# First attention of a two-layer kernel: quadrant matmuls in two pairs per segment, elu made up to a segment ahead

## The chip, the cores and the metric

The kernel runs on one core of a Trainium2 chip. The metric is the device time of one execution in microseconds (us). Timed runs of the kernel before gave 761.18, 761.67 and 762.66 us; the median is 761.67. The engines are called PE (TensorE, matmuls; PEld is its weight load), DVE (VectorE), ACT (ScalarE), POOL (GpSimd) and SP (SyncE, which issues DMAs).

## What is computed

Two layers on x of shape 4 x 512 x 128. Each is `x = x + attention(layernorm(x)) * silu(experts(layernorm(x)))`. The change concerns the attention of the first layer alone: 16 heads of 64, sequences cut into segments of 64 positions, with a memory M, Z carried from segment to segment:

```
scores = where(mask, -inf, q @ k^T / 8);   att_dot = softmax(scores) @ v
sq = elu(q) + 1;   att_mem = sq @ M / (sq @ Z^T)
sk = elu(k) + 1;   M += sk^T @ v;   Z += sum(sk)
out = (gate * att_mem + (1 - gate) * att_dot) @ Wo
```

q, k and v are projections of the normed x. There are 4 batches of 8 segments, so 32 segments, all 16 heads of a segment at once.

## The kernel before

A first stage norms x and runs the first layer's experts (to about 78 us). Then comes the first attention, `attn0`, until about 339 us, into which the beginning of the second layer's experts is woven (the `between` table: sums, norms, transposes `lnt`, hidden layer `pgr` and router logits `lp` after segments 18 to 23, and the first expert's `ph` in segment 31). The second layer's experts and its attention follow to the end.

**Order.** Matmuls, activations and DVE operations are pinned: each of these engines runs them in the order in which the program emits them. POOL operations and DMAs are not pinned; a scheduler places those. So the loop at the end of `attn0` is the order of PE, ACT and DVE, written by hand.

**Segment n.** The steps, each with its PSUM tile's name, which is also its name in the profile:

- `scores(n)`: 16 quadrant products (64 x 64) into `sc`; DVE takes the minimum with the causal cap into E (L656); `scores_exp` is the exponential on ACT.
- `elu_exp(n, w)`: ACT makes exp and relu of q (w = 0) or k (w = 1), 128 x 512 each (`elu`, `up`); `elu(n, w)`: DVE joins the two (L679).
- `memory(n)`: sq times memory, quadrants, into `mm`; DVE divides (L711, L712), POOL multiplies by the gate (L731).
- `update(n)`: sk times v, quadrants, into `mu`; DVE adds to the memory `mz` (L746). The last segment of a batch has none.
- `attend(n)`: E times v, quadrants, into `dot`; DVE divides and keeps the extremes of the sums (L765, L712, L768); POOL multiplies by the gate and adds the memory's part (L769, L770).
- `keys(n)`: four 128 x 128 transposes of elu(k) into `pk` (L686); ACT copies them to `sk`.
- `attended(n)`: four transposes of the result into `pa` (L780); ACT copies them in four parts to `attT`.
- `output(h)`, once in four segments: 32 products with Wo into `po`; DVE multiplies by the expert branch (`sg`, L802), POOL adds to x (L803).
- `values(n)`: two gathers from DRAM bring v into one of four buffers `vone`.

**Projections.** `project(h)` makes q, k and v of four segments in 12 chunks: four of v (`pv`, two products 128 x 512; ACT evicts to `vt`, of two buffers, DVE in the first two projections; SP stores `vt` to DRAM), then four of k and four of q (`pp`, 128 rows by 64 columns, eight products; ACT evicts to `pj`). The loop deals them out, three per segment (four in segments 0 to 2). A profile counts twice as many PE instructions as products, since these are in f32.

**PSUM.** `wide` tiles (two banks, three buffers) hold sc, mm, mu, dot and po; `narrow` tiles (one bank, two buffers) hold pp, pv, pk, pa and, from the woven-in work, lnt, pgr and lp. A matmul group that reuses a buffer waits for its eviction.

**Array shapes.** sc, mm, mu and dot use a 64 x 64 quarter of the array; pk, pa, pv and lnt the whole of it; pp 128 rows by 64 columns; po 64 rows by 128 columns.

The loop before, per segment: PE runs sc of the next segment, the output if it is due, a chunk, mm, a chunk, mu, a chunk, pk of the next segment, dot, pa of the segment before.

Of the kernel before, what the change touches and what calls it, by code (L numbers as in the profile page):

```python
# [101 lines left out]
def bc(ap, axis, n):  # L102

    shape = list(ap.shape)
    return ap.unsqueeze(axis).to_broadcast(shape[:axis] + [n] + shape[axis:])


class Kernel:
# [454 lines left out]
    def attn0(self, xnT, g0, stack, psum, between):  # L563
# [25 lines left out]
        def wide(name):  # L589

            return psum.tile([P, 2, S], F32, name=name, tag="w", bufs=3)
# [47 lines left out]
        def blocks(n, w):  # L639
            s = n % 4  # L640
            return qkv[n // 4][w][:, s * 8 : s * 8 + 8, :]

        def scores(n):

            q, k = blocks(n, 0), blocks(n, 1)
            ps = wide(f"sc{n}")
            for hp in range(4):
                for p in range(2):
                    for a in range(2):
                        self.mm1(  # L650
                            ps[halves[a], p, hp * 64 : hp * 64 + 64],
                            lhsT=k[halves[p], 2 * hp + a, :], rhs=q[halves[p], 2 * hp + a, :],
                            start=True, stop=True,
                        )
            e = pool.tile([P, 2, 4, LSEG], F32, name=f"E{n}", tag="E")
            self.vec1(nc.vector.tensor_tensor(  # L656
                e, ps[:, :, 0:256].rearrange("p x (hp c) -> p x hp c", hp=4),
                bc(bc(self.cap, 1, 4), 1, 2), ALU.min,
            ))
            seg[n]["e"] = e  # L660

        def scores_exp(n):
            e = seg[n]["e"]
            self.act1(e, e, AF.Exp, scale=1.0 / math.sqrt(DK))

        def last(n):
            return n % 8 == 7

        def elu_exp(n, w):
            t = pool.tile([P, 8, 64], F32, name=f"elu{w}{n}", tag=f"elu{w}")  # L670
            up = pool.tile([P, 8, 64], F32, name=f"up{w}{n}", tag="up")
            self.act1(t, blocks(n, w), AF.Exp)
            self.act1(up, blocks(n, w), AF.Relu)
            seg[n][w] = t, up

        def elu(n, w):

            t, up = seg[n][w]
            self.vec1(nc.vector.scalar_tensor_tensor(t, t, 1.0, up, ALU.min, ALU.add))  # L679
            seg[n][w] = t  # L680

        def turn(n, src, name):

            ps = narrow(f"{name}{n}").rearrange("p (hp c) -> p hp c", hp=4)
            for hp in range(4):
                self.pin(nc.tensor.transpose(  # L686
                    ps[:, hp], src[:, 2 * hp : 2 * hp + 2, :].rearrange("d a j -> d (a j)"),
                    self.ident,
                ))
            return ps.rearrange("p hp (x d) -> p hp x d", x=2)  # L690

        def keys(n):
            t = pool.tile([P, 4, 2, DK], F32, name=f"sk{n}", tag="sk")
            self.act1(t, turn(n, seg[n][1], "pk"), AF.Copy)
            seg[n]["sk"] = t

        def values(n):

            for p in range(2):
                src = vd[n // 4][p].rearrange("(s hp r) d -> s r hp d", s=4, hp=4)  # L700
                nc.sync.dma_start(out=vone[n % 4][:, :, p, 0:DK], in_=src[n % 4])

        def heads(ps):

            return ps[:, :, 0 : 4 * (DK + 1)].rearrange("p x (y v) -> p x y v", v=DK + 1)
# [4 lines left out]
        def divided(ps, t, r, sums):  # L710
            self.vec1(nc.vector.reciprocal(r, sums))  # L711
            self.vec1(nc.vector.tensor_tensor(t, heads(ps)[:, :, :, 0:DK], bc(r, 3, DK), ALU.mult))  # L712

        def memory(n):


            mz, sq = self.mz[(n % 8 + 1) % 2 + 1 if n % 8 else 0], seg[n][0]
            ps = wide(f"mm{n}")
            for hp in range(4):
                for p in range(2):  # L720
                    for a in range(2):
                        at = (2 * a + hp // 2) * (DK + 1)
                        self.mm1(
                            ps[halves[(a + hp) % 2], p, at : at + DK + 1],
                            lhsT=sq[halves[p], 2 * hp + a, :], rhs=mz[halves[p], hp, a, :],
                            start=True, stop=True,
                        )
            t = seg[n]["t1"] = pool.tile([P, 4, 2, DK], F32, name=f"t1{n}", tag="t1")
            r = pool.tile([P, 2, 4], F32, name=f"rm{n}", tag="rm")
            divided(ps, t.rearrange("p hp y d -> p y hp d"), r, heads(ps)[:, :, :, DK])  # L730
            nc.gpsimd.tensor_mul(t, t, self.gate)  # L731
# [16 lines left out]
        def attend(n):  # L748


            e, v = seg[n]["e"], vone[n % 4]
            ps = wide(f"dot{n}")
            for u in range(2):
                for p in range(2):
                    for hp in (2 * u, 2 * u + 1):
                        for a in range(2):
                            at = (2 * u + p) * (DK + 1)
                            self.mm1(
                                ps[halves[(a + hp) % 2], a, at : at + DK + 1],
                                lhsT=e[halves[a], p, hp, :], rhs=v[halves[a], hp, p, :],  # L760
                                start=True, stop=True,
                            )
            both = pool.tile([P, 2, 2, 4], F32, name=f"rd{n}", tag="rd")
            sums = both[:, 0]
            self.vec1(nc.vector.tensor_scalar_max(sums, heads(ps)[:, :, :, DK], SUM_MIN / 2))  # L765
            t = pool.tile([P, 4, 2, DK], F32, name=f"t2{n}", tag="t2")
            divided(ps, over(t), both[:, 1], sums)
            self.vec1(nc.vector.tensor_tensor(self.sums0, both, self.sums0, ALU.max))  # L768
            nc.gpsimd.tensor_mul(t, t, gate2)  # L769
            nc.gpsimd.tensor_add(t, t, seg[n]["t1"])  # L770
            seg[n]["att"] = t

        def attended(n):

            if n % 4 == 0:

                attT[n // 4] = pool.tile([P, 16, 4, 32], F32, name=f"attT{n}", tag="attT")
            ps = narrow(f"pa{n}").rearrange("p (hp c) -> p hp c", hp=4)
            for hp in range(4):
                self.pin(nc.tensor.transpose(  # L780
                    ps[:, hp, :], seg[n]["att"][:, hp].rearrange("i p v -> i (p v)"),
                    self.ident,
                ))
            src = ps.rearrange("p (a u) (h t c) -> p c a u h t", a=2, h=2, c=16)
            dst = attT[n // 4][:, :, n % 4].rearrange("p c (u y t) -> p c u y t", u=2, y=4)
            for h in range(2):
                for a in range(2):
                    self.act1(dst[:, :, :, (a + h) % 2 * 2 + a], src[:, :, a, :, h], AF.Copy)
# [16 lines left out]
        nseg = 8 * B  # L805
        for n in range(nseg):
            seg[n] = {}
        todo = project(0)
# [11 lines left out]
        scores(0)  # L820
        scores_exp(0)
        elu(0, 0)
        for n in range(nseg):
            if n == 0 or n % 4 == 3:
                todo = project((n + 1) // 4 + 1)
                each = 3 if n else 4
            nxt = n + 1 < nseg
            more = nxt and not last(n + 1)
            if n + 2 < nseg:
                values(n + 2)  # L830
            if more:
                elu_exp(n + 1, 1)
            if nxt:
                scores(n + 1)
            if n % 4 == 1 and n > 4:
                output(n // 4 - 1)
            for chunk in todo[:1]:
                chunk()
            if more:
                elu(n + 1, 1)  # L840
            if nxt:
                scores_exp(n + 1)
            memory(n)
            for chunk in todo[1:2]:
                chunk()
            if nxt:
                elu_exp(n + 1, 0)
            if not last(n):
                update(n)
            if nxt:  # L850
                elu(n + 1, 0)
            for chunk in todo[2:each]:
                chunk()
            todo = todo[each:]
            if more:
                keys(n + 1)
            for f, *args in between.get(n - 0.5, []):
                f(*args)
            attend(n)
            if n:  # L860
                attended(n - 1)
            for f, *args in between.get(n, []):
                f(*args)
        return [lambda: attended(nseg - 1), lambda: output(2 * B - 1)]
# [1411 lines left out]
```

## Time and profile before

| | |
|---|---|
| median of three runs | 761.67 us |
| profiled execution | 761.59 us, its span on the core 759.8 us |
| PE busy | 723.9 us (95%) |
| DVE, ACT, POOL busy | 515.0, 494.5, 294.7 us |
| stage of segments 3 to 18 (115.76 to 238.06 us) | PE 120.63, DVE 74.39, ACT 86.90, POOL 68.85 us busy of 122.30 |
| segments 27 to 30 (310.90 to 334.73 us) | PE 18.22, DVE 20.37, ACT 14.51, POOL 16.64 us busy of 23.83 |
| mean granted PE clock | 0.992 |

A profile line of a group gives start, duration, engine, line, operation, output and inputs, the array rows and columns or the tile's shape, how many instructions, and in brackets how long the engine had stood idle and what ended that. L331 and L334 are helpers through which all matmuls and activations go, so groups are told by their tiles. PE ends are modelled and matmuls overlap: the distance between starts of successive groups is the time that a group takes on PE. In a table of stretches the columns are the stretch, its length, busy time (and count) of PE, PEld, DVE, ACT and POOL, then the granted clock, the DMA share and GB/s.

### The profile page before, as it was taken

How to read it: one execution, taken by the hardware profiler on the slowest of the kernel's cores; microseconds unless marked ns; L12 is line 12 of the kernel's file. 1: busy time of each engine (PE TensorE's matmuls, PEld its weight loads, DVE VectorE, ACT ScalarE, POOL GpSimd, SP SyncE). 2: the span in 40 equal slices, each digit the busy share in tenths (PEclk: the TensorE clock that was granted, in tenths of full speed). 3: DMA queues.
4: the chain of work that ended last, by engine and by line, in shares of the span. 5: the costliest groups of instructions: out<-in, count | busy, mean ns of one | idle time of the engine just before them, and what ended most of it. 6: DMA issues, size and time to landing. Idle time of an engine off the chain costs nothing.

```text
span 759.8 us, 23585 instructions
## 1 busy us (share of the span) xinstructions
PE 723.9 (95%) x10044; PEld 436.8 (57%) x10044; DVE 515.0 (68%) x1126; ACT 494.5 (65%) x800; POOL 294.7 (39%) x340
## 2 busy tenths in 40 slices
PE   8999899999999989889999999999999999999995
PEld 4666677787876857667576777433234424432244
DVE  7766375556557755874365643688888998777874
ACT  4432567668567775742433222998999799989860
POOL 7660055546555543673007004331152344140160
PEclk9999999999999998999999999999999999999999
DMA  7830423223132221100002550667684776759200
GB/s 192 149 89 0 112 87 100 58 62 97 42 89 73 57 72 31 45 3 1 1 1 71 180 127 1 138 198 185 129 233 153 167 167 199 190 123 222 56 16 17
DMA packets 77743, 74.71 MB, mean 98 GB/s; under 512 B 41936, under 2 KB 66800, under 8 KB 74560
## 3 DMA queue, kind: packets, MB, share of 16 engines
q1 hardware_dynamic: 75568, 71.98, 36.5%
q0 software_dynamic: 1488, 0.90, 0.9%
q8 instruction: 81, 1.33, 0.8%
q10 hardware_dynamic: 576, 0.26, 0.1%
q14 instruction: 30, 0.25, 0.1%
HBM read 50.04 MB, written 23.07 MB: 96 GB/s over the span
## 4 chain that ended last, share of the span: by engine, by line
PE 75%; ACT 11%; DVE 9%; DMA 2%; issue 1%; POOL 0%; SPq 0%; DVEq 0%; ACTq 0%
PE eo L331 10%; PE acc L331 9%; PE pp L331 8%; ACT e L334 7%; PE ph L331 7%; PE po L331 6%; PE s L331 3%; PE b L331 3%; PE pl L331 3%; PE pv L331 2%; PE pa L780 2%; PE mm L331 2%; PE dot L331 2%; PE mu L331 2%; PE den L331 2%; PE pg L331 2%
## 5 line engine op out<-in xcount | busy, mean ns | idle before, releaser
L334 ACT ACTIVATE e<-s 128x1024 f32<-128x1024 f32 x126 | 124.3, 1062 | 12.7 <-PE s L331 12.1
L331 PE MATMUL acc<-e,strip 128*32 128x512 f32 x1008 | 124.6, 598 | 0.3 <-DVE e L1710 0.3
L334 ACT ACTIVATE e<-e 128x1024 f32<-128x1024 f32 x106 | 109.7, 1099 | 0.0
L334 ACT ACTIVATE h<-ph 128x1024 f32<-128x1024 f32 x32 | 32.7, 1023 | 85.5 <-PE ph L331 85.5
L769 POOL TENSOR_TENSOR t<-t,gate 128x512 f32<-128x512 f32 x32 | 40.8, 1274 | 75.0 <-DVE sums L768 67.5
L331 PEld LDWEIGHTS acc<-e,strip 128*32 128x32 f32 x1008 | 28.5, 109 | 69.9 <-issue 59.2
L331 PEld LDWEIGHTS eo<-w_out,h 128*128 128x128 f32 x512 | 60.7, 192 | 12.5 <-issue 9.7
L334 ACT ACTIVATE pj<-pp 128x512 f32<-128x512 f32 x64 | 38.3, 598 | 41.2 <-PE pp L331 40.9
L331 PE MATMUL eo<-w_out,h 128*128 128x128 f32 x512 | 63.4, 277 | 1.6 <-DVE g L966 1.3
L679 DVE SCALAR_TENSOR_TENSOR elu<-elu,up 128x512 f32<-128x512 f32 x60 | 48.2, 804 | 20.4 <-ACT up L334 20.3
L331 PE MATMUL ph<-xnT,w_in 128*128 128x512 f32 x128 | 61.2, 600 | 0.0
L966 DVE SCALAR_TENSOR_TENSOR g<-eo,gw,g 128x128 f32<-128x128 f32 x112 | 31.5, 343 | 40.0 <-PE eo L331 40.0
L731 POOL TENSOR_TENSOR t<-t,gate 128x512 f32<-128x512 f32 x32 | 41.4, 1294 | 40.6 <-DVE t L712 40.5
L770 POOL TENSOR_TENSOR t<-t,t 128x512 f32<-128x512 f32 x32 | 46.1, 1441 | 2.5
L331 PE MATMUL s<-q,k 64*128 64x512 bf16 x256 | 40.8, 382 | 4.5 <-ACT e L334 2.9
L331 PEld LDWEIGHTS <-k 64*128 64x128 bf16 x256 | 8.8, 94 | 61.0 <-issue 59.1
L1550 POOL TENSOR_TENSOR pr<-pr,pr 128x512 f32<-128x512 f32 x14 | 22.6, 1636 | 41.8 <-DVE pr L1545 41.8
L334 ACT ACTIVATE elu<-pj 128x512 f32<-128x512 f32 x60 | 38.0, 633 | 0.1
L334 ACT ACTIVATE up<-pj 128x512 f32<-128x512 f32 x60 | 37.8, 631 | 0.0
L334 ACT ACTIVATE attT<-pa 128x128 f32<-128x128 f32 x128 | 25.1, 284 | 17.6 <-PE pa L780 17.6
L331 PE MATMUL pv<-l0Wv,xnT 128*128 128x512 f32 x64 | 35.6, 652 | 0.8 <-ACT vt L334 0.7
L331 PE MATMUL pp<-xnT,l0Wk 128*64 128x128 f32 x512 | 35.1, 283 | 0.7 <-ACT g L334 0.7
(290 smaller groups left out, 1520.7 us busy)
## 6 DMA issues: line engine op xcount, KB each, us to landing
vd<-vt SPq DMA_DIRECT2D x32, 256.0 KB
vone<-vd SPq DMA_DIRECT2D x64, 128.0 KB
first<-qe SPq DMA_DIRECT2D x8, 1024.0 KB
second<-qf SPq DMA_DIRECT2D x16, 512.0 KB
third<-qf SPq DMA_DIRECT2D x32, 256.0 KB
qf<-qT SPq DMA_DIRECT2D x64, 64.0 KB
k<-kd SPq DMA_DIRECT2D x16, 256.0 KB
q<-qd SPq DMA_DIRECT2D x16, 256.0 KB
```

The source lines that it names most:

```text
L331: return self.pin(self.nc.tensor.matmul(*args, **kw))
L334: return self.pin(self.nc.scalar.activation(*args, **kw))
L679: self.vec1(nc.vector.scalar_tensor_tensor(t, t, 1.0, up, ALU.min, ALU.add))
L731: nc.gpsimd.tensor_mul(t, t, self.gate)
L769: nc.gpsimd.tensor_mul(t, t, gate2)
L770: nc.gpsimd.tensor_add(t, t, seg[n]["t1"])
L780: self.pin(nc.tensor.transpose(ps[:, hp, :], seg[n]["att"][:, hp].rearrange("i p v -> i (p v)"), self.ident,))
L966: self.vec1(v.scalar_tensor_tensor(acc[b][:, k, :], eo[:, k, :], w, acc[b][:, k, :], ALU.mult, ALU.add))
L1550: self.nc.gpsimd.tensor_add(self.prod1[b, m], self.prod1[b, m], t)
```

## The change

Only the preamble and the loop of `attn0` change; no operation is added or dropped.

- mm of a segment follows sc of the next one at once, and dot follows mu at once: two pairs of quadrant groups.
- The two groups of transposes (pk, pa) come next, and the projection chunks beyond the first come last. The first chunk stays between mm and mu.
- The output moves behind that first chunk.
- Chunks per segment become 4, 4, 3, 1 (for n mod 4 = 3, 0, 1, 2) instead of 3 each.
- The exponential and relu of k are issued at the end of the segment two before, those of q at the start of the segment before; DVE's elu of k comes between E and the division of mm, elu of q right behind that division, ahead of the update's addition.

```diff
         elu(0, 0)
+        elu_exp(1, 1)
         for n in range(nseg):
             if n == 0 or n % 4 == 3:
                 todo = project((n + 1) // 4 + 1)
-                each = 3 if n else 4
+            each = 4 if n < 3 else (4, 3, 1, 4)[n % 4]
...
-            if more:
-                elu_exp(n + 1, 1)
             if nxt:
+                elu_exp(n + 1, 0)
                 scores(n + 1)
-            if n % 4 == 1 and n > 4:
-                output(n // 4 - 1)
-            for chunk in todo[:1]:
-                chunk()
             if more:
                 elu(n + 1, 1)
+            memory(n)
+            for chunk in todo[:1]:
+                chunk()
             if nxt:
                 scores_exp(n + 1)
-            memory(n)
-            for chunk in todo[1:2]:
-                chunk()
+            if n % 4 == 1 and n > 4:
+                output(n // 4 - 1)
             if nxt:
-                elu_exp(n + 1, 0)
+                elu(n + 1, 0)
             if not last(n):
                 update(n)
-            if nxt:
-                elu(n + 1, 0)
-            for chunk in todo[2:each]:
-                chunk()
-            todo = todo[each:]
-            if more:
-                keys(n + 1)
             for f, *args in between.get(n - 0.5, []):
                 f(*args)
             attend(n)
+            if more:
+                keys(n + 1)
             if n:
                 attended(n - 1)
+            for chunk in todo[1:each]:
+                chunk()
+            todo = todo[each:]
+            if n + 2 < nseg and not last(n + 2):
+                elu_exp(n + 2, 1)
             for f, *args in between.get(n, []):
                 f(*args)
```

More of the change, by code (lines that the diff above doesn't have):

```diff
@@ L830, in attn0 @@
                 values(n + 2)
+            if nxt:
+                elu_exp(n + 1, 0)
+                scores(n + 1)
             if more:
-                elu_exp(n + 1, 1)
+                elu(n + 1, 1)
+            memory(n)
+            for chunk in todo[:1]:
+                chunk()
             if nxt:
-                scores(n + 1)
+                scores_exp(n + 1)
             if n % 4 == 1 and n > 4:
                 output(n // 4 - 1)
-            for chunk in todo[:1]:
-                chunk()
-            if more:
-                elu(n + 1, 1)
             if nxt:
-                scores_exp(n + 1)
-            memory(n)
-            for chunk in todo[1:2]:
-                chunk()
-            if nxt:
-                elu_exp(n + 1, 0)
+                elu(n + 1, 0)
             if not last(n):
                 update(n)
-            if nxt:
-                elu(n + 1, 0)
-            for chunk in todo[2:each]:
-                chunk()
-            todo = todo[each:]
-            if more:
-                keys(n + 1)
             for f, *args in between.get(n - 0.5, []):
```

## The prediction

> **What bounds the kernel now.** The page first: where the time goes and whether the clock is whole.
>
> ```profile
> PE 723.9 (95%) x10044; PEld 436.8 (57%) x10044; DVE 515.0 (68%) x1126; ACT 494.5 (65%) x800; POOL 294.7 (39%) x340
> PEclk9999999999999998999999999999999999999999
> PE 75%; ACT 11%; DVE 9%; DMA 2%; issue 1%; POOL 0%; SPq 0%; DVEq 0%; ACTq 0%
> ```
>
> TensorE (PE) is busy nearly all the time and carries the chain. The first attention runs from about 92 to 339 us. Next, its timeline on PE: what counts is the distance from one group's start to the next one's, since matmuls overlap.
>
> ```profile
> 219.25 0.70 PE L331 MATMUL dot<-vone,E 64*64 64x65 f32 x32
> 219.88 0.66 PE L780 MATMUL pa<-ident,t 128*128 128x128 f32 x4
> 220.47 0.69 PE L331 MATMUL sc<-pj,pj 64*64 64x64 f32 x32
> 221.41 3.84 PE L331 MATMUL po<-l0wo,attT 64*128 64x128 f32 x64 [0.25 <-ACT attT L334]
> 225.18 1.09 PE L331 MATMUL pp<-xnT,l0Wk 128*64 128x128 f32 x16
> 226.21 0.70 PE L331 MATMUL mm<-mz,elu 64*64 64x65 f32 x32
> 226.83 1.09 PE L331 MATMUL pp<-xnT,l0Wk 128*64 128x128 f32 x16
> 227.86 0.70 PE L331 MATMUL mu<-vone,sk 64*64 64x65 f32 x32
> ...
> 262.83 0.66 PE L780 MATMUL pa<-ident,t 128*128 128x128 f32 x4
> 263.33 0.60 PE L900 MATMUL lnt<-ident,xn 128*128 128x128 f32 x4
> ...
> 310.90 0.69 PE L331 MATMUL sc<-pj,pj 64*64 64x64 f32 x32
> 311.41 0.65 PE L331 MATMUL mm<-mz,elu 64*64 64x65 f32 x32
> 311.88 0.69 PE L331 MATMUL mu<-vone,sk 64*64 64x65 f32 x32
> ```
>
> PE has next to no gaps here, so its own order is the bound. A quadrant group (64*64) takes 0.63 when another array shape follows (mm 226.21 to 226.83), but 0.51 and 0.47 when a quadrant group follows (310.90, 311.41, 311.88). Transposes: 0.59 before a quadrant group, 0.50 before another transpose (262.83 to 263.33). Elsewhere in this timeline pp takes 1.02 before another shape and 0.92 before pp; pv 1.06 and 0.96. A change of shape costs **0.09 to 0.14 us**. Third, the clock, where PE is thin, because it is cut to half after such stretches (282.9 to 289.7 and 334.1 to 337.5):
>
> ```profile
> 279.50:282.90 3.40, 2.25 (x32) 1.91 (x25) 2.38 (x7) 2.10 (x7) 1.65 (x2) 1.00 0.65 198
> 317.05:320.46 3.41, 1.89 (x76) 1.47 (x69) 3.31 (x7) 2.18 (x5) 2.73 (x2) 1.00 0.06 13
> 330.70:334.10 3.40, 1.55 (x77) 1.30 (x68) 3.07 (x7) 1.67 (x3) 2.84 (x3) 1.00 0.00 0
> ```
>
> The second number is PE's busy time: 1.55 of 3.40 brought the half clock, 1.89 did not; 2.25 did, much of it in router matmuls of 32 rows by 8 columns. Last, the releases on ACT and DVE:
>
> ```profile
> 244.49 0.60 ACT L334 ACTIVATE vt<-pv 128x512 f32<-128x512 f32 x1 [1.30 <-DMA vd<-vt]
> ```
> ```profile
> 320.90 1.49 DVE L679 SCALAR_TENSOR_TENSOR elu<-elu,up 128x512 f32<-128x512 f32 x1
> ```
>
> The evictions of v have two buffers and can wait for their store; an elu on DVE takes 1.49 instead of 0.69 when POOL multiplies at the same time.
>
> **What the Trainium skill says.** "TensorEngine Tiling (Array Packing)", Tiling Modes: changing the tiling mode, not just the tile, drains TensorE. The trace agrees, at 0.09 to 0.14. "DMA: Bandwidth & Descriptors", Anatomy of one DMA: about 2.0 us fixed per transfer, plus the bytes (there for transfers issued by GpSimd). Here the 24 stores of v from ACT (256 KB each, issued by SP) had their last packet 1.65 to 3.65 after issue, mean 2.15. "GPSIMD Engine Reference", Key points: GpSimd shares its SBUF interfaces with VectorE and contends with DVE instructions of two SBUF inputs. That is the elu at 1.36 to 1.50, while E, t and mz, which read PSUM, stay at 0.69.
>
> **The change part by part.** Call the segments of one projection S3, S0, S1, S2 (n mod 4 = 3, 0, 1, 2). Per segment, in order, with | for a change of shape: before, S0 is sc|v|mm|k|mu|k|pk|dot|pa|; after, sc mm|k|mu dot|pk pa|k k k|. Over the four segments 36 changes become 19, at about 0.1 each.
>
> *The pairs and runs alone.* With the distances above, S3 is sc 0.515, mm 0.626, v 1.056, mu 0.487, dot 0.626, pk 0.495, pa 0.495, v 0.962 twice, v 1.056 = 7.28 (6.79 where the memory's last segment has no update). S0 with pp is 7.23; S1 with the output matmuls (3.772) and two trailing chunks 10.08; S2, one chunk, 4.36 (3.87 where no keys follow). S3 and S2 occur in both forms in eight segments: 7.28 + 6.79 + 2x7.23 + 2x10.08 + 4.36 + 3.87 = 56.9. Before, eight segments take 61.15 (sc at 115.76, 176.91 and 238.06). So −4.2, in which the 0.32 that po waits for attT is gone too: mm and a chunk stand before it now.
>
> *What gives it back.* (1) pk, pa and the first trailing chunk share two PSUM buffers ("t"), so that chunk needs pk's buffer. sk starts 0.693 after pk and takes 0.597, so the chunk starts 1.35 after pk, not 0.99 (v) or 1.08 (pp): +0.36 and +0.27. Before, dot and others lay between. In eight segments 2x0.36 + 4x0.27 = 1.8. (2) S2 is so short that att(n−1), which takes POOL 1.28 + 1.3 to 1.6 after t2 on DVE, comes 0.5 to 1 late for pa of S3, and elu on DVE meets these POOL operations; walking the queues, S3 becomes 7.90 and 7.48: +0.6 over (1). (3) The last three v now come at 0.96, so the fourth eviction waits for the second one's store: vt2 starts 1.81 before the next sc, ends 0.6 later, +2.15 makes 0.95 after sc, against 0.11 without a wait. Behind it on ACT stand elu_exp of k (2 operations), of q (2), the chunk's pj, E and sk, issued 0.52 apart (elu_exp) or 0.50: sk starts at 0.95 + 0.5 + 4x0.52 + 2x0.5 = 4.55 and is done at 5.15, so the trailing chunks of S0 start at 5.2, and S0 takes 8.07 instead of 7.50: +0.57, twice. (4) The rest stays covered. One segment's operations need 4.6 on DVE (five at 0.62, the small ones 0.24, 0.20, 0.24, 0.17 and a wait) and on ACT 3.7 plus 0.5 per chunk, below PE's 7 except in S2. elu of k, now ahead of the division of mm, waits for ACT until 1.8 after sc, and pk needs it at 3.28; were it later than that, PE would wait as long. The output's sg on DVE now holds up elu of q, mz and the sums of dot until po ends (6.05 after sc); they end at 8.7, before the next sc at 10.35; its POOL addition finds POOL idle. So nothing for these.
>
> Together 56.9 + 1.8 + 0.6 + 1.1 = **60.4 against 61.15**. In n = 3 to 18 that is twice 0.7: **−1.4**.
>
> *n = 19 to 26 (72.84 us before).* At n = 22 two chunks and their changes leave, but xnT waits behind the elu_exp placed ahead of it: 9.22 becomes 7.3. At n = 23 three v now run before the router matmuls, which wait for v's buffers: 10.8 becomes 11.0. The rest as above: 7.9 + 8.07 + 10.9 + 7.3 + 11.0 + 8.07 + 10.35 + 4.36 = 67.95; the half clock cost 2.7 here (sc 1.06, pv 2.0, mm 1.08, pp 1.84 instead of 0.63, 1.06, 0.63, 1.02) and, the router matmuls being as thin as before, I leave it: 70.65, **−2.2**.
>
> *n = 27 to 30 (310.90 to 334.73, no chunks).* DVE bounds it: 5.93 per segment without a gap, two elu at 1.36 and 1.49. The pairs give nothing here. But elu of q now follows t1 at once and starts before POOL takes up that t1, so it runs first: about 0.8 instead of 1.49. 5.2 for a segment; walked through 4.97, 5.2, 7.6 (output), 4.1 = 21.9: **−2.0**. PE is then busy above half of the last window before 334, as in the one at 317, so I take the second half-clock spell as gone: **−1.7** (pa, mm and ph lost that).
>
> *n = 0 to 2.* mm(0) no longer has a v chunk ahead of it while elu of q is made (1.0 idle), and DVE, which evicts these v, is late: +0.8; then −0.2 for two segments: **+0.6**. SP's stores and gathers of v keep their number; a gather ahead of a store of v1 would delay it by up to 1 us, which the third v's slack covers. The elu_exp(1,1) ahead of the loop is the same two operations, made while ACT would wait for the next scores: nothing, or 1.0 if they delayed elu of q.
>
> Sum: −1.4 − 2.2 − 2.0 − 1.7 + 0.6 = −6.7, from the profiled 761.59 (span 759.8, 1.8 around it; the median 761.67 is 0.08 off): **755**.
>
> **Bounds of the unknown.** pk before pa and chunk before po were not in the trace: 0.495 to 0.59 and 1.02 to 1.03, 0 to +1.5 us in all; I take the low end. The half clock: both spells gone is 752.3, both kept 756.7, one more window +1.7. Wait (3): 0.2 to 1.9 per S0 and six of them, −2 to +8.
>
> **Rivals.** *Full gain.* If ACT and the stores keep up, 4.2 counts instead of 0.7 per eight segments: 3.5 more in each of three, 755 − 10.5 = 744.5. For it: ACT is busy 87 of 122 us. Against it: sk's 1.29 after pk is the same in nearly every segment. *All given back.* Waits (1) to (3) a little larger, both spells kept: 760 to 763. *Slower.* The v stores, in a burst right after the gathers of values, all take what the slowest of 24 took, 3.65: ACT's whole queue behind the fourth v is 1.5 later in each of six S0, 755 + 9 = 764. It decides from about 3.2 on: 1.1 us times six is the 6.7 gained. One of 24 was that slow.
>
> **How the numbers follow.** Forecast 0.60 (751 to 759), full gain 0.12, given back 0.14, slower 0.14. 0.2% (1.5 us) is about what can be told from no change here. Range 747.5 to 762.5: it leaves out half of the full gain and most of the slower case. Faster 0.74, same 0.13, slower 0.13.
>
> **What would show it.** On PE: sc to mm 0.51, mu to dot 0.49; first chunk after pa 1.35 after pk's start, waiting for ACT; vt waiting for the DMA in every S3, and S0 near 8.0; eight segments in 60 to 61 us. Wrong if eight segments take under 58 (the buffers don't bind) or over 62; if segments 27 to 30 still take 5.9; or if half-clock spells appear elsewhere.

## The result, and the profile after

The changed kernel takes **758.15 us** in the median of 12 runs (756.70 to 760.22), the kernel before 761.57 beside it: ratio 0.9962, 95% interval 0.9946 to 0.9979. It is faster by 0.4%, about half of the 6.7 us that the forecast took off. The profiled execution took 758.95 us, its span 757.1.

The page of the changed kernel: PE's busy time and share of the chain fall, those of DVE and ACT in the chain rise.

```profile
PE 710.7 (94%) x10044; PEld 430.8 (57%) x10044; DVE 507.6 (67%) x1126; ACT 492.2 (65%) x800; POOL 299.5 (40%) x340
PE 68%; ACT 15%; DVE 13%; DMA 2%; issue 2%; SPq 0%; DVEq 0%; ACTq 0%
```

PE's timeline for segment 12 of the changed kernel (n mod 4 = 0):

```profile
186.02 0.69 PE L331 MATMUL sc<-pj,pj 64*64 64x64 f32 x32
186.54 0.65 PE L331 MATMUL mm<-mz,elu 64*64 64x65 f32 x32
187.11 1.09 PE L331 MATMUL pp<-xnT,l0Wk 128*64 128x128 f32 x16
188.14 0.70 PE L331 MATMUL mu<-vone,sk 64*64 64x65 f32 x32
188.65 0.65 PE L331 MATMUL dot<-vone,E 64*64 64x65 f32 x32
189.61 0.66 PE L686 MATMUL pk<-ident,elu 128*128 128x128 f32 x4 [0.31 <-DVE elu L679]
190.49 0.63 PE L780 MATMUL pa<-ident,t 128*128 128x128 f32 x4 [0.23 <-ACT pj L334]
191.41 2.89 PE L331 MATMUL pp<-xnT,l0Wk 128*64 128x128 f32 x48 [0.28 <-ACT sk L334]
194.22 0.70 PE L331 MATMUL sc<-pj,pj 64*64 64x64 f32 x32
```

The pairs are about as short as read from before: sc to mm 0.52, mu to dot 0.51. The price stands in brackets on the next three lines; the last line is the start of segment 13, so this segment took 8.20. ACT's timeline around it says where the price comes from:

```profile
185.17 0.60 ACT L334 ACTIVATE vt<-pv 128x512 f32<-128x512 f32 x1 [0.26 <-PE pv L331]
187.19 0.60 ACT L334 ACTIVATE vt<-pv 128x512 f32<-128x512 f32 x1 [1.42 <-DMA vd<-vt]
...
190.76 0.59 ACT L334 ACTIVATE sk<-pk 128x512 f32<-128x512 f32 x1
```

The fourth eviction of v (187.19) stands 1.42 us for the store of the second one, and everything behind it on ACT is late: elu of k (so pk waits), pj (so pa waits), sk (so the chunks wait).

The span by stretches, cut at the starts of sc (and of mm of segment 31), in us:

| stretch | before | forecast | after |
|---|---|---|---|
| up to the first sc | 91.91 | 91.91 | 92.42 |
| segments 0 to 2 | 23.84 | 24.4 | 25.90 |
| segments 3 to 18 | 122.31 | 120.9 | 119.80 |
| segments 19 to 26 | 72.83 | 70.65 | 70.61 |
| segments 27 to 30 | 23.83 | 21.8 | 22.69 |
| the rest | 425.03 | 423.3 | 425.70 |

The first and the last stretch vary by themselves: over the 17 profiles of this document the first took 90.9 to 94.7 us and the last 423.7 to 425.7. The changed kernel's profile has one spell of half clock, 3.4 us long, in each of the two (from 11.4 and from 332.2 us); the kernel before had none in the first. What the change itself did is read from the four rows between.

### The profile page after: what moved, and what is told of

Its sections match the earlier page's. It is cut to its first block, busy times and chain, and to the rows that moved or that the text cites. A ratio compares the mean times of both kernels' runs of the same rounds, so it can differ in the third digit from the quotient of the medians.

```text
span 757.1 us, 23560 instructions
## 1 busy us (share of the span) xinstructions
PE 710.7 (94%) x10044; PEld 430.8 (57%) x10044; DVE 507.6 (67%) x1126; ACT 492.2 (65%) x800; POOL 299.5 (40%) x340
## 4 chain that ended last, share of the span: by engine, by line
PE 68%; ACT 15%; DVE 13%; DMA 2%; issue 2%; SPq 0%; DVEq 0%; ACTq 0%
PE eo L331 10%; PE acc L331 9%; PE pp L331 7%; ACT e L334 7%; PE ph L331 7%; PE po L331 5%; PE s L331 3%; PE b L331 3%; PE pl L331 3%; PE den L331 2%; PE pg L331 2%; PE pv L331 2%; DVE elu L679 2%; DMA vd<-vt 2%; PE pu L331 2%
## 5 line engine op out<-in xcount | busy, mean ns | idle before, releaser
L731 POOL TENSOR_TENSOR t<-t,gate 128x512 f32<-128x512 f32 x32 | 49.6, 1549 | 82.8 <-DVE t L712 82.8
L656 DVE TENSOR_TENSOR E<-sc,cap 128x512 f32<-128x512 f32 x32 | 22.0, 687 | 44.6 <-PE sc L331 44.6
L769 POOL TENSOR_TENSOR t<-t,gate 128x512 f32<-128x512 f32 x32 | 40.7, 1272 | 26.8 <-DVE sums L768 23.4
L770 POOL TENSOR_TENSOR t<-t,t 128x512 f32<-128x512 f32 x32 | 43.0, 1343 | 2.5
L331 PEld LDWEIGHTS <-k 64*128 64x128 bf16 x256 | 8.8, 94 | 61.1 <-issue 59.3
L334 ACT ACTIVATE sk<-pk 128x512 f32<-128x512 f32 x28 | 16.7, 598 | 31.6 <-PE pk L686 31.3
L331 PE MATMUL pp<-xnT,l0Wq 128*64 128x128 f32 x512 | 32.9, 277 | 2.8 <-ACT sk L334 1.7
```

Source lines behind the costliest of these rows:

```text
L331: return self.pin(self.nc.tensor.matmul(*args, **kw))
L334: return self.pin(self.nc.scalar.activation(*args, **kw))
L656: self.vec1(nc.vector.tensor_tensor(e, ps[:, :, 0:256].rearrange("p x (hp c) -> p x hp c", hp=4), bc(bc(self.cap, 1, 4), 1, 2), ALU.min,))
```

## The experiments

All ratios are to the kernel before, run beside. Each kernel starts from the changed kernel unless another is named; each diff is against the kernel that it starts from. A and B are the two theories of the expectation just above. "Segments 0 mod 4" are those with n mod 4 = 0, and a segment's time runs from its sc to the next one's. Where medians of different kernels are set against each other, the changed kernel's is 758.15.

**Four buffers for v.**

```diff
-                t = pool.tile([P, S], F32, name=f"vt{h}_{p}_{k}", tag="vt")
+                t = pool.tile([P, S], F32, name=f"vt{h}_{p}_{k}", tag="vt", bufs=4)
```

> Changed kernel with four buffers for the evicted v (vt) instead of two; nothing else. Theory A (the fourth eviction of v waits for the store of the second, and the queue behind it on ACT makes each segment n mod 4 = 0 long): that wait on the DMA goes, segments 4, 8, 12, 16, 20 fall from 8.0 to 8.2 us to 7.5 to 7.6, the whole by about 3 us, to 755. Rival B (those segments are long because pk, pa and chunks share two PSUM buffers, ACT would catch up anyway): the DMA wait goes, the segments stay at 8.0 or above, the whole within 0.5 us of 758.2.

752.41 us, ratio 0.9892 (0.9872 to 0.9911). PE's timeline for segment 12:

```profile
182.64 0.69 PE L331 MATMUL sc<-pj,pj 64*64 64x64 f32 x32
...
185.85 0.66 PE L686 MATMUL pk<-ident,elu 128*128 128x128 f32 x4
186.34 0.60 PE L780 MATMUL pa<-ident,t 128*128 128x128 f32 x4
187.19 2.88 PE L331 MATMUL pp<-xnT,l0Wk 128*64 128x128 f32 x48 [0.25 <-ACT sk L334]
190.01 0.69 PE L331 MATMUL sc<-pj,pj 64*64 64x64 f32 x32
```

Two of the three brackets are gone with the store's wait; the 0.25 for sk, wait (1) of the prediction, stays. Segments 4, 8, 12, 16 and 20 take 7.37 instead of 8.0 to 8.2, 3.6 us in all. A holds. The gain is larger than expected: segment 23 is shorter too (11.01 to 10.28), and segment 2 by 0.3. Of the remaining 1.0 of the 5.7 us between the medians, 0.6 is what the kernel before, run beside, differed too.

**The same in the kernel before.**

> Kernel before with four buffers for the evicted v instead of two. Theory A (the wait for the store is made by the change, which puts three v chunks in a row; before, they stood apart): in the kernel before it is worth only the waits of pa after ACT's vt, 0.33, 0.33, 0.99 and 0.55 us, so 1 to 2.5 us, to about 759.5. Rival B (two buffers cost the kernel before as much as the changed one): it falls by 5 us, to 756.

756.42, ratio 0.9943 (0.9923 to 0.9963). Segments 3 to 18 stay at 122.28, so there the change makes the wait, as A says. But the whole falls by 0.6%, as B says: segment 19 falls from 7.73 to 6.69, 23 from 10.78 to 9.46, 24 from 9.44 to 8.18, the last two partly since the profile shows no half clock there. A's amount was too small.

**First three segments as before.** The loop takes the old body for n < 3, elu placement included.

```diff
+            if n < 3:
...
+                scores(n + 1)
+                for chunk in todo[:1]:
+                    chunk()
...
+                memory(n)
...
+                continue
```

> Changed kernel with segments 0, 1 and 2 in the order of before (elu placement too), from segment 3 on as changed. Theory A (the 2.05 us that the first three segments lose are local: mm has no chunk ahead of it, DVE evicts v late, and sc of segment 4 follows the last chunk of q at once and waits for its eviction): sc of segment 0 to sc of segment 4 takes 23.9 us again instead of 25.9, the whole falls by 2.0, to 756. Rival B (what is lost there is only moved from later waits): the whole stays within 0.5 us of 758.2.

756.91, ratio 0.9944 (0.9927 to 0.9961). The stretch takes 23.79 again, as A says; the whole fell by 1.2 us and not by 2.0. The changed kernel's PE timeline shows the three waits that this took away:

```profile
94.53 1.00 PE L331 MATMUL mm<-mz,elu 64*64 64x65 f32 x32 [0.95 <-DVE elu L679]
...
101.43 1.13 PE L331 MATMUL pv<-l0Wv,xnT 128*128 128x512 f32 x2 [1.36 <-DVE vt L616]
...
118.32 0.69 PE L331 MATMUL sc<-pj,pj 64*64 64x64 f32 x32 [0.70 <-ACT pj L334]
```

**Woven-in DVE work moved.**

```diff
-                    18: [(first.sums, 0)], 19: [(first.sums, 1)],
+                    13: [(first.sums, 0)], 17: [(first.sums, 1)],
...
-                    23: [(first.logits, 0), (first.logits, 1), (first.chosen, 0)],
+                    23: [(first.logits, 0), (first.logits, 1)], 24.25: [(first.chosen, 0)],
...
+            for f, *args in between.get(n - 0.75, []):
+                f(*args)
             if n % 4 == 1 and n > 4:
```

> Changed kernel with three pieces of woven-in DVE work moved: the norm sums of batches 0 and 1 from segments 18 and 19 to 13 and 17, the choice of experts of batch 0 from segment 23 to ahead of the output in segment 25. Theory A (dot, now close behind sc, waits for DVE's minimum of the next scores to free a PSUM buffer, and DVE is late by that work): the waits of 0.87, 0.42 and 1.37 us of dot in segments 19, 21 and 24 go, segments 19 to 26 take about 68 us instead of 70.6, the whole falls by 2 to 2.6, to 756. Rival B (DVE is as late wherever the work stands): segments 13, 17 and 25 grow by as much, the whole stays at 758.2.

756.85, ratio 0.9949 (0.9930 to 0.9968). These were the waits in the changed kernel's PE timeline:

```profile
241.83 0.70 PE L331 MATMUL dot<-vone,E 64*64 64x65 f32 x32 [0.87 <-DVE E L656]
...
289.45 0.70 PE L331 MATMUL dot<-vone,E 64*64 64x65 f32 x32 [1.37 <-DVE E L656]
```

Segment 19 falls from 8.98 to 7.95, and 13 and 17 do not grow, so A there. In segment 24 dot no longer waits either, but a spell of half clock fell on it in this profile (8.88). The wait in segment 21 stayed, for the division of mm and not for E: there A was wrong. Segment 27 grew by 0.44. The whole fell by 1.3 us, less than the 2 to 2.6 expected.

**Trailing chunks ahead of the transposes.**

```diff
+            for chunk in todo[1:each]:
+                chunk()
+            todo = todo[each:]
             if more:
                 keys(n + 1)
             if n:
                 attended(n - 1)
-            for chunk in todo[1:each]:
-                chunk()
-            todo = todo[each:]
```

> Changed kernel with the trailing chunks ahead of the two groups of transposes instead of behind them; as many changes of array shape. Theory A (whatever follows in the two PSUM buffers waits for ACT: the wait of 0.25 for sk goes, but pa now waits for the last chunk's eviction, 0.3 us, and where that is v, for its store too, over 1 us): no gain, segments 3 mod 4 near 8.3, 0 mod 4 near 7.5, the whole 757.5 to 760. Rival B (the wait for sk is the loss, worth 0.25 to 0.36 in each of 18 segments): the whole falls by 3 to 5 us.

772.95, ratio 1.0147 (1.0126 to 1.0167): far worse than either expected. PE and ACT in segment 7:

```profile
161.91 0.63 PE L780 MATMUL pa<-ident,t 128*128 128x128 f32 x4 [2.31 <-ACT vt L334]
```
```profile
161.17 0.60 ACT L334 ACTIVATE vt<-pv 128x512 f32<-128x512 f32 x1 [2.27 <-DMA vd<-vt]
```

A's direction holds: in PSUM, pa stands behind the fourth v, so PE waits for the store itself, 1.8 to 2.3 in segments 3, 7, 11 and 15 and not a good 1; segments 3 mod 4 from 3 to 19 take 9.7 to 10.05. In the first attention this profile has half clock at 129, 163, 228 and from 300 to 306 us, each time after 3.4 us in which PE was busy for only 1.0 to 1.8; the changed kernel's has it at 332 us alone. In the changed kernel's order ACT waits for the store, 1.42 in segment 12, and PE pays only 0.6 to 0.8 of it.

**pk in a wide PSUM tile.**

```diff
-            ps = narrow(f"{name}{n}").rearrange("p (hp c) -> p hp c", hp=4)
+            ps = (
+                wide(f"{name}{n}")[:, 0] if 3 < n < 28 and n % 4 != 3 else narrow(f"{name}{n}")
+            ).rearrange("p (hp c) -> p hp c", hp=4)
```

> Changed kernel in which the transposes pk that trailing chunks follow (segments 3 to 26, not n mod 4 = 2) go into a wide PSUM tile, so that the first trailing chunk finds a free narrow one. Theory A (wait 1 of the prediction: the chunk starts 1.35 after pk because it needs pk's buffer, and PE loses that time): the chunk starts 1.05 after pk, the wait of 0.25 for sk goes in some 18 segments, the whole falls by 3 to 5 us, to 754. Rival B (ACT, as late as before, makes the next wait: the second chunk or the next sc waits instead): the wait moves, the whole stays within 1 us of 758.2.

759.57, ratio 0.9977 (0.9964 to 0.9989): no gain. The wait for sk is gone, but in segments 0 mod 4 pk now waits:

```profile
158.56 0.63 PE L688 MATMUL pk<-ident,elu 128*128 128x128 f32 x4 [1.09 <-DVE t L714]
```

DVE's division of mm, which frees pk's buffer, stands behind the elu of k that is late. So B in the outcome, though the wait moved to pk and not to one of the groups that B names. Segments 1 mod 4 gain 0.2 each, those 0 mod 4 nothing.

**Three chunks each.**

```diff
-            each = 4 if n < 3 else (4, 3, 1, 4)[n % 4]
+            each = 4 if n < 3 else 3
```

> Changed kernel with three chunks in every segment from 3 on, as before, instead of 4, 4, 3, 1. Theory A (the burst of three v after the transposes makes the store wait; with two in a row and the fourth v as the next segment's first chunk the store has 3 us): segments 0 mod 4 have no DMA wait, the four segments of a projection take about 29.4 us instead of 29.9, the whole 755 to 756.5. Rival B (4, 4, 3, 1 is worth something itself, since fewer changes of shape remain): the whole is 760 or more.

754.19, ratio 0.9909 (0.9894 to 0.9923). A for the whole and for its cause: no eviction waits for a store, and segments 0 mod 4, with a chunk fewer, take 6.48. But A's amount isn't there: the four segments of a projection take 29.85 (119.38 for segments 3 to 18) and not 29.4. The gain stands in segments 19 to 26 (68.66) and 27 to 30 (21.19).

**Filled idle time.**

```diff
             attend(n)
+            if n in (27, 28, 30):
+                pd = narrow(f"pd{n}")
+                for k in range(8 if n == 30 else 4):
+                    self.pin(nc.tensor.transpose(pd[:, k % 4 * P : k % 4 * P + P], self.ident, self.ident))
```

> Changed kernel with additional transposes of the identity, read by nobody, after dot in segments 27 and 28 (four) and 30 (eight): work that changes no result, put where PE waits 0.6, 0.6 and 1.3 us. Theory A (the spell of half clock at 332 us comes from PE's idle time there): the spell goes, ph of segment 31 takes 2.8 us or less instead of 3.5, the whole falls by 1 to 2 us. Rival B (the spell comes from elsewhere, or falls by the phase of the clock's window, not by this idle time): a spell of 3.4 us still stands between 320 and 340 us and the whole stays within 0.7 us of 758.2, or rises by that.

758.02, ratio 0.9958 (0.9943 to 0.9972). First the changed kernel, then this one:

```profile
330.26 0.66 PE L780 MATMUL pa<-ident,t 128*128 128x128 f32 x4 [1.28 <-POOL t L770]
...
332.04 3.61 PE L331 MATMUL ph<-xnT,w_in 128*128 128x512 f32 x4
```
```profile
329.15 1.09 PE L854 MATMUL pd<-ident 128*128 128x128 f32 x8
...
332.30 1.98 PE L331 MATMUL ph<-xnT,w_in 128*128 128x512 f32 x4
```

In this profile the spell at 332 us is gone and ph takes 1.98, as A says. The total doesn't show it (0.1 us), as B says; one spell stands at 286.7 us instead. So the idle time matters, but it is not enough by itself: the kernel with four buffers has the same idle time in its tail, and its profile has no spell. The points on the clock at the end come back to this.

**Early elu alone**, in the kernel before: elu of k made a segment ahead and elu of q at a segment's start, PE's order untouched.

> Kernel before with PE's order and chunks as they were and only the elu of q and k made as early as in the changed kernel (on ACT and DVE). Theory A (the gain is in PE's order; elu was late only in segments 27 to 30, where DVE is full anyway, and an elu of q that starts ahead of POOL's multiplication runs undisturbed): segments 27 to 30 fall by about 1 us, the rest stays, the whole is 760.5. Rival B (the early elu is worth as much as the order): the whole falls by 2 us or more, to 759.5 or less.

765.25, ratio 1.0070 (1.0042 to 1.0098): slower than before, which neither theory said. PE's and ACT's timelines in segment 7:

```profile
154.90 0.63 PE L780 MATMUL pa<-ident,t 128*128 128x128 f32 x4 [0.97 <-ACT vt L334]
```
```profile
154.16 0.60 ACT L334 ACTIVATE vt<-pv 128x512 f32<-128x512 f32 x1 [1.57 <-DMA vd<-vt]
```

The early elu, too, makes an eviction of v wait for a store. Segments 3 to 18 take 125.11 instead of 122.31, and segment 0 takes 9.58 instead of 8.65.

**Order alone**, changed kernel with the elu of before.

```diff
-        elu_exp(1, 1)
...
+            if more:
+                elu_exp(n + 1, 1)
             if nxt:
-                elu_exp(n + 1, 0)
                 scores(n + 1)
...
             if nxt:
-                elu(n + 1, 0)
+                elu_exp(n + 1, 0)
             if not last(n):
                 update(n)
+            if nxt:
+                elu(n + 1, 0)
...
-            if n + 2 < nseg and not last(n + 2):
-                elu_exp(n + 2, 1)
```

> Changed kernel with the changed order of PE and chunks, but elu placed as before (exp and relu of k at the start of the segment ahead, of q after the scores' exponential, DVE's elu of q behind the update). Theory A (ACT has the same operations ahead of sk either way, DVE has room except in segments 27 to 30): segments 3 to 26 within 1 us of the changed kernel's 190.4, segments 27 to 30 up by about 1 to 23.7, the whole 758 to 760. Rival B (the early elu is what lets the pairs stand close: mm waits for elu of q otherwise): segments 3 to 26 up by 3 us or more, the whole over 761.

763.53, ratio 1.0029 (1.0017 to 1.0042). B, and my own theory A fell:

```profile
151.06 0.70 PE L331 MATMUL mm<-mz,elu 64*64 64x65 f32 x32 [0.76 <-DVE rd L765]
...
163.62 2.88 PE L331 MATMUL pp<-xnT,l0Wk 128*64 128x128 f32 x48 [0.71 <-ACT sk L334]
```

mm, now right behind sc, waits for the elu of q (the DVE operation ahead of rd), and sk has two more operations ahead of it on ACT. Segments 3 to 18 take 123.10.

**Both crossed with four buffers**, to tell the store's wait from the rest.

> PE's order of before with the early elu, and four buffers for the evicted v. Theory A (the early elu alone is slow because elu operations that stood between two evictions of v, and covered the store, are gone): the wait for the store goes, segments 3 to 18 take 122.3 us as in the kernel before instead of 125.1, the whole is 755.5 to 757, as the kernel before with four buffers (756.4). Rival B (the early elu delays evictions on ACT by itself): segments 3 to 18 stay over 124, the whole over 759.

> Changed order of PE with the elu placement of before, and four buffers for the evicted v. Theory A (what the late elu costs is apart from the stores: sk stands behind two more operations on ACT, so trailing chunks wait 0.6 to 0.7 instead of 0.25, and mm waits for elu of q in the segment after a short one): segments 0 mod 4 fall by the store's wait, those 3 mod 4 stay near 8.9 and 8.7, segments 3 to 18 take about 120.5, the whole is 758 to 760. Rival B (with the store's wait gone ACT is in time with either placement): the whole is as the changed kernel with four buffers, 752 to 753.

756.97, ratio 0.9941 (0.9925 to 0.9957), and 760.91, ratio 1.0000 (0.9986 to 1.0014). For segments 3 to 18, with four buffers:

| | elu as before | early elu |
|---|---|---|
| PE's order of before | 122.28 | 122.29 |
| changed order | 122.36 | 116.85 |

A in the first: in these segments the early elu alone costs only by the store (segment 0 takes 9.59 here too, so what it loses there has another cause). The second is nearer A than B, but at 760.91 above A's 758 to 760, and the stretch takes 122.36 and not 120.5. Its waits for elu of q and for sk are still there without the store's:

```profile
147.75 0.70 PE L331 MATMUL mm<-mz,elu 64*64 64x65 f32 x32 [0.77 <-DVE rd L765]
...
160.19 2.89 PE L331 MATMUL pp<-xnT,l0Wk 128*64 128x128 f32 x48 [0.62 <-ACT sk L334]
```

Neither part is worth anything alone in this stretch; together they are worth 5.4 us.

**The edits together.** Four buffers, first segments as before and woven-in work moved; the same with pk wide; the same three with three chunks each.

> Changed kernel with four buffers for the evicted v, segments 0 to 2 in the order of before, and the woven-in DVE work moved (the three edits that were tried singly). Theory A (each removes its own wait): their gains add, 5.3 + 1.4 to 2 + 1.1 us, the whole about 750. Rival B (the same waits are only counted three times): the whole stays at 752.

> The same with the transposes pk in a wide PSUM tile where chunks trail them. Theory A (with two v buffers that wait only moved to DVE, because elu of k was late behind the fourth v; with four buffers pk finds the division of mm done and the trailing chunk starts 0.25 to 0.35 earlier in 18 segments): 3 to 5 us below the three edits, about 746. Rival B (pk waits for DVE's division of mm in any case): within 1 us of the three edits.

> The three edits (four buffers, segments 0 to 2 in the order of before, woven-in work moved) and three chunks in every segment. Theory A (4, 4, 3, 1 loses only by the store's wait; without it, it saves changes of shape and lets two of eight segments be short): this is 1 to 3 us slower than the three edits alone (748.2), 749.5 to 751. Rival B (three each is better in itself, by its full segments): under 747.5.

748.22, ratio 0.9825 (0.9811 to 0.9838); 747.03, ratio 0.9816 (0.9802 to 0.9829); 749.56, ratio 0.9846 (0.9831 to 0.9862). The gains of the three add, as A says, which expected 750. pk in a wide tile adds 1.2 at most, and the two intervals overlap: nearer B, since pk still waits for the division of mm (0.24 in segment 8, 0.92 in segment 11). Without the store's wait, 4, 4, 3, 1 is ahead of three each by 1.3 us, within A's 1 to 3, though these intervals touch as well. Segments 3 to 18 take 116.72 against 119.39, partly returned in segments 27 to 30 (23.32 against 21.32).

## Why the prediction was wrong, point by point

The direction and the time within the range were right; the size was not: 6.7 us forecast, 3.4 measured (2.6 between the two profiles). The failed steps are terms of its sum. By the table of stretches, three of them promised 4.7 us more than came: the clock term (−1.7 forecast, +0.7 in "the rest"), n = 0 to 2 (+0.6, it was +2.05) and n = 27 to 30 (−2.0, it was −1.1). The stretch up to the first sc, where the forecast had nothing, took 0.5 more, and n = 3 to 18 gave 1.1 more than promised.

- **Pairs and runs alone, −4.2 in eight segments: right, and slightly more.** With four buffers eight segments take 58.4 (116.85 in sixteen), where the sum has 56.9 + 1.8 + 0.6 for waits (1) and (2) = 59.3. The walk gave the second group of a pair 0.63, as if it stood alone between two other shapes; it takes 0.58 (mm above, 186.54 to 187.11). pa ahead of sc takes 0.53 and not 0.59 (177.38 to 177.91 in the changed kernel).
- **Waits (1) to (3): right in kind.** (1) The chunk starts 1.34 after pk (185.85 to 187.19 above). (2) pa of segment 7 stands 0.43 until 151.82; POOL's addition for it ends at 151.76. (3) Segments 0 mod 4 took 8.0 to 8.2 against 8.07. Segments 3 to 18 gained 2.5 instead of 1.4, because most came out under the walk: segments 1 mod 4 took 10.23 against 10.35, those 2 mod 4 3.80 and 4.23 against 3.87 and 4.36, and segment 3, which follows a long segment 2 and so has no wait (2), 7.45 against 7.90.
- **"n = 0 to 2 ... +0.6": mis-sized, it was +2.05.** The idle mm (0.95) was as forecast. Missed: sc of segment 4 follows the last chunk of q at once and waits 0.70 for its eviction, a true dependence that the old order covered by keys, dot and pa. Too small: DVE's evictions of v came later, behind an elu of 1.39, and pv waited 1.36 for them. The early elu in the old order lengthened this stretch by 0.9 as well (24.78).
- **"I take the second half-clock spell as gone: −1.7": it stood** from 332.25 us, and ph took 3.61. The step that failed is that PE would be busy above half of the last window. It was busy for 1.63 of the 3.41 us before the spell, because pa stood 1.28 for POOL there and mm 0.50 for mz. The term was also the wrong kind of thing, as the next point shows.
- **Where the spells fall.** In all 17 profiles the clock changes only at whole multiples of 3.413 us from one another (before: 282.91, 289.74, 334.11 and 337.52). So there are fixed windows of this length, and where they begin against the program differs from profile to profile. In the tails (segments 27 to 31) half clock followed windows with PE busy for 1.56 (before), 1.63 (changed), 1.70 (old start) and 1.81 us (early elu alone), and did not follow 1.74 (three chunks each) or 1.83 (the three edits). With four buffers the idle stretch fell on two windows, 320.31 to 323.73 with 2.35 and 323.73 to 327.14 with 2.71, and no spell came. Of all places where the windows could begin, about a third leave 1.70 or less in one window, in this tail as in that of the kernel before with four buffers (an estimate from these two traces). With the idle time filled, no place leaves less than 2.51. So the change hardly altered the chance of the spell, and the forecast took one profile's spell for the kernel's.
- **The border and the price of a spell.** Outside the tails the border on PE's busy time is not the same: 2.81, some of it in router matmuls, was followed by half clock in the kernel with filled idle time (283.27 to 286.68), and 1.57 was not with the chunks ahead of the transposes (101.53 to 104.94). As for the price: over 32 runs of the kernel before, mean granted clock 0.988 to 0.998, the time rises by 0.54 us per us of clock withheld (time times one minus the clock; correlation 0.75). A spell of 3.4 us withholds 1.7, so it costs about 0.9 in the mean by this estimate; in the 12 runs of the changed kernel the slope is only 0.26, with a correlation of 0.31, so the amount is loose.
- **"n = 19 to 26 ... −2.2": the sum right by two errors, so by luck.** The half clock that I left in (2.7) wasn't there in this profile, and the segments took 2.65 more than walked. Most of that is in waits of dot: 0.87 in segment 19, 0.42 in segment 21, 1.37 in segment 24. In 19 and 24 dot's buffer needs E of the next scores, and DVE comes to E late behind norm sums (19) and the choice of experts (24). The walk has "The rest as above" here and so left out DVE's woven-in work; with dot 2.6 after sc instead of about 5.5 (183.60 to 189.17 before), that work is no longer covered.
- **"n = 27 to 30 ... −2.0": it was −1.1.** The segments were 5.15, 5.31, 7.59 and 4.64 against 4.97, 5.2, 7.6 and 4.1: after POOL's late att(29) mm of segment 31 waits another 0.50 for mz on DVE.
- **Rivals.** Full gain needed the stores to keep up. With four buffers they do, and the changed kernel is then at 752.4, not 744.5. Of these 7.9 us waits (1) and (2), which stay, explain about 4.5 (an estimate: 58.4 against 56.9 in eight segments, three times); the rest is in the terms above. The slower case named the right mechanism, the store, but not its size. ACT waited for it, 1.12 to 1.53 us, at the fourth v of each of the six projections from segment 3 on; in segment 12 from the store's issue to the eviction that it held up were 2.25 us (184.94 to 187.19), near the 2.15 of the forecast and not 3.65, and it cost 0.6 to 0.8 in each of the five segments from 4 to 20.

What stays open: how often the clock is really cut in a given tail, since each kernel has one profile, what sets the border of PE's busy time elsewhere, and the gap of 0.39 us in dot of segment 11, for which the profile names no releaser.

## What to carry to other kernels

Before grouping like matmuls, list for every buffer what now lies between its writer and the next one who needs it: work that separated them was cover, for an eviction, a store or a true dependence. A reordering and the earlier inputs that it needs can each be worth nothing, or less, alone (122.28, 122.29, 122.36) and 4.4% of the stretch together (116.85), so try them crossed. And when a wait appears on ACT, follow what is queued behind it before counting a loss on PE: one extra pair of buffers for v, given to the kernel before, was worth as much as the reordering (ratios 0.9943 and 0.9962, with intervals that overlap), and without it the reordering kept only part of its gain.

## What the runs showed of the hardware

A change of array shape costs 0.09 to 0.14 us on PE by the distances of the kernel before. In the changed kernel sc and mm as a pair take 1.09 (186.02 to 187.11), where apart they took 0.63 each: 0.16 for two changes fewer. An elu on DVE that starts ahead of POOL's multiplication takes 0.68 (146.32 us) and POOL's takes 1.66 beside it (146.48); L731 went from 1294 to 1549 ns in the mean, while the mean of all elu stayed at 804 and 805. Stores of 256 KB took 1.65 us and more from issue to last packet in the kernel before; with v chunks in a row ACT stood 1.42 us for one in the changed kernel, and 2.27 where the chunks stood ahead of the transposes.
